# Causal attention and a ternary feed-forward layer on one core: the layout in which K and Q are kept in DRAM, and where some loads stand in the queue

## The chip, the core and the metric

The kernel runs on one core of one Trainium2 chip, as one program with one launch. The metric is the device time of that program in microseconds: the median of several executions. One further execution is recorded by the hardware profiler; its page and its trace are what the prediction is argued from.

## The reference

The input is one sequence of 4096 tokens with 256 features. There are 16 heads of 16 features each, causal. All is float32.

```python
xn  = layernorm(x) * gamma + beta
q, k, v = split(xn @ w_qkv.T)                 # each 4096 x 256, 16 heads of 16
sim = (q * 16**-0.5) @ k.T                    # per head, masked above the diagonal
x   = layernorm(x + softmax(sim) @ v)         # heads side by side again
h   = silu(x @ w1.T * s1) * (x @ w2.T * s2)   # 256 -> 1024
h   = gelu(h @ h1.T * sh1)                    # 1024 -> 1024
h   = gelu(h @ h2.T * sh2)                    # 1024 -> 1024
out = layernorm(x + h @ w3.T * s3)            # 1024 -> 256
```

The feed-forward weights are ternary (times a constant); the scales s1, s2, sh1, sh2 (1024 numbers each) and s3 (256) multiply each output feature.

## The kernel before

**Precision.** [...] A value that has to keep its precision is split into a high part (the rounded value) and a low part (what the rounding left out), and a product is the sum of high times high, low times high and high times low. For a head, K and Q have 16 rows (features) each, so one matmul does all three products at once when the rows are stacked: for Q the rows are high, low, high; for K they are high, high, low. That is 48 rows. Two more rows hold ones for K and, for Q, the negative row maximum as a high and a low row (called hl), so that the maximum is subtracted inside the scores' matmul. With them there are 50 rows (`KR`).

**Stages.** The tokens are cut into 8 blocks of 512. `projections` makes Q, K and V of a block and stores them in DRAM: `qaug[b]` (16 heads x 48 rows x 512 tokens), `kaug[b]` (16 x 50 x 512) and `vaug[b]`. The high part is stored twice, since it stands in the stack twice; line 269 issues these stores, three of 16 rows for each half of the heads. Line 274 stores K's two rows of ones. For block 0 the stores go around over three queues (ACT, SP, POOL), afterwards all are issued by POOL.

**Attention.** For each query block (in the order 0, 1, 2, 3, 4, 6, 7, 5) and each group of four heads (`qd`) there is a step. `row_max` goes over the key blocks once for the maxima: matmuls at line 442, and VectorE's reduction at line 453. Its last part, `rows`, turns the maxima and writes the hl rows into the Q tile with four small DMAs (line 469). `scores` goes over the key blocks a second time: matmuls at line 486, the exponential on ScalarE at line 490. `product` multiplies with V at line 504. The two passes run interleaved, the maxima some steps ahead.

Both passes read their K tiles from DRAM through `fetch`. A K tile has 128 partitions: two halves of 64, each with two heads side by side along its free dimension, and of each half the first 50 rows are filled, by one DMA from SP's queue (line 410). For the scores a V tile comes along (line 416). The tiles of the maxima are called mk, those of the scores sk, and there are two buffers of each, so that one tile is read while the next is loaded. The Q tile (qt, line 429) is loaded once for a step, 48 rows to each half.

**Feed-forward.** While attention goes on, the feed-forward layer of finished blocks is worked off in pieces between the attention matmuls: `feed`, with up to two blocks at work, started by `start(b)`. `start` loads the block's x (line 672, tile x1) and its attention output (line 681), and lets `total` add them some turns later. Weight tiles (wt, line 665) are loaded through POOL's queue. The last block goes through `closing` when attention is done.

**Order.** The order of the instructions on TensorE, VectorE, ScalarE and POOL is that of the program text, fixed by `in_order` with dependencies that carry no wait. DMA issues are left out of that order: the scheduler places them by itself, and one that waits for nothing can move ahead. A dependency added by `after` holds one instruction behind another in the same way, without a wait between them on the chip. The scales are loaded by `scales()`, called in the text just before attention starts; on the chip these loads stand among SP's first, at 1.83 us, and so do the x1 load of block 0 (10.16 us) and the eight stores of ones (from 11.39 us).

Of the kernel before, what the change touches and what calls it, by code (L numbers as in the profile page):

```python
# [7 lines left out]
F32 = mybir.dt.float32  # L8
FR = mybir.dt.float32r
AF = mybir.ActivationFunctionType  # L10
ALU = mybir.AluOpType
# [4 lines left out]
N, E, H, D = 4096, 256, 16, 16  # L16
# [4 lines left out]
B = 512  # L21
NB = N // B
NQ = H // 4
KR = 50
# [19 lines left out]
def tokens(ap):  # L44
    return ap.rearrange("(t p) e -> p t e", p=P)


class Layer:
    def __init__(self, tc, a):
        self.tc, self.nc, self.a = tc, tc.nc, a  # L50
        self.last = {}

    def pool(self, ctx, name, bufs=1, **kw):
        return ctx.enter_context(self.tc.tile_pool(name=name, bufs=bufs, reuse_waits="tile", **kw))
# [20 lines left out]
    def chain(self, key):  # L75
# [3 lines left out]
            self.after(inst, self.last[key])  # L79
        self.last[key] = inst.name  # L80

    def run(self):
        tc, nc, a = self.tc, self.nc, self.a
        with ExitStack() as ctx:
            dram = self.pool(ctx, "dram", space=DRAM)
            cst = self.pool(ctx, "cst")
            self.small = self.pool(ctx, "small", 4)
            self.qaug = [dram.tile([H, 48, B], F32, name=f"qaug{b}") for b in range(NB)]
            self.kaug = [dram.tile([H, KR, B], F32, name=f"kaug{b}") for b in range(NB)]
            self.vaug = [dram.tile([NQ, P, 4, 4, D + 1], F32, name=f"vaug{b}") for b in range(NB)]  # L90
            self.attn = [dram.tile([B, E], F32, name=f"attn{b}") for b in range(NB)]

            self.ident = cst.tile([P, P], F32, name="ident")
            make_identity(nc, self.ident)
            self.mhalf = cst.tile([P, 4], F32, name="mhalf")
            nc.gpsimd.memset(self.mhalf, -0.5)
            self.wbad = cst.tile([P, 22], F32, name="wbad")
            self.wseq = (
                [("glu", g, 0) for g in range(4)]
                + [(n, g, k) for n in ("h1T", "h2T") for g in range(4) for k in range(2)]  # L100
                + [("w3T", 0, k) for k in range(2)]
            )
            self.sc = {}
            for n in ("w1_s", "w2_s", "h1_s", "h2_s"):
                self.sc[n] = cst.tile([P, 8], F32, name=n)
            self.w1_half = cst.tile([P, 8], F32, name="w1_half")
            self.w12 = cst.tile([P, 8], F32, name="w12")
            self.s3 = cst.tile([P, E], F32, name="s3")

            own = mybir.EngineType  # L110
            with ExitStack() as fctx, self.in_order(own.PE, own.DVE, own.Activation, own.Pool):
                self.layer(fctx)
            bad = self.verdict(cst)
            with tc.If(bad > 0), ExitStack() as gctx:
                self.general(gctx)

    def scales(self):
        for n, t in self.sc.items():
            self.nc.sync.dma_start(t, self.a[n].rearrange("(c p) -> p c", p=P))
        self.nc.gpsimd.tensor_scalar(self.w1_half, self.sc["w1_s"], 0.5, None, ALU.mult)  # L120
        self.nc.gpsimd.tensor_tensor(self.w12, self.w1_half, self.sc["w2_s"], ALU.mult)
        s3 = self.a["w3_s"].rearrange("(o f) -> o f", o=1)
        self.nc.sync.dma_start(self.s3, s3.broadcast_to([P, E]))

    def norm_steps(self, dst, src):

# [73 lines left out]
    def projections(self, ctx):  # L200
# [5 lines left out]
        one = self.pool(ctx, "p1", side="right")  # L206
        wk = self.pool(ctx, "pw", 2, side="right")

        def fetch(b):
            xb = wk.tile([P, 4, E], F32, name="xb")  # L210
            nc.sync.dma_start(xb, tokens(a["x"][b * B : (b + 1) * B]))
            return xb

        def front(b, xb):
# [37 lines left out]
        for b in range(NB):  # L252
            xh, xl = parts.pop(b)
            prods = [(wh, xh, c) for c in range(2)] + [(wl, xh, c) for c in range(2)] + [(wh, xl, c) for c in range(2)]
            for off, dst, order in ((E, self.kaug, (0, 0, 1)), (0, self.qaug, (0, 1, 0))):
                kp = ps.tile([P, 2, B], F32, name="s", tag="s", bufs=3)
                for T in range(2):
                    for n, (wp, xp, c) in enumerate(prods):
                        nc.tensor.matmul(  # L259
                            kp[:, T], wp[:, c, off + T * P : off + (T + 1) * P], xp[:, c], start=n == 0, stop=n == 5  # L260
                        )
                kh = wk.tile([P, 2, B], FR, name="kh")
                nc.scalar.copy(kh, kp)
                kl = wk.tile([P, 2, B], FR, name="kl")
                nc.vector.tensor_tensor(kl, kp, kh.bitcast(F32), ALU.subtract)
                for n, (i, g) in enumerate(sorted((i, g) for g, i in enumerate(order))):
                    for T in range(2):
                        queues = (nc.scalar, nc.sync, nc.gpsimd) if b == 0 else (nc.gpsimd,)
                        queues[(2 * n + T) % len(queues)].dma_start(
                            dst[b][8 * T : 8 * T + 8, 16 * g : 16 * g + 16, :], (kh, kl)[i][:, T].bitcast(F32)  # L270
                        )
                yield 12 * MM, True
                if dst is self.kaug:
                    nc.sync.dma_start(self.kaug[b][:, 48:KR, :], ones)
                    if b + 1 < NB:
                        yield from front(b + 1, xb)
                        if b + 2 < NB:
                            xb = fetch(b + 2)
            if b + 2 < NB:
                self.layernorm(xb, xb)  # L280
            v = vst[b % 2]
            vps = ps.tile([P, 4, E], F32, name="s", tag="s", bufs=3)
            for t in range(4):
                for n, (wp, xp, c) in enumerate(prods):
                    nc.tensor.matmul(
                        vps[:, t], xp[:, c, t * P : (t + 1) * P], wp[:, c, 2 * E :], start=n == 0, stop=n == 5
                    )
            for t in range(4):
                nc.scalar.copy(v[:, :, t, :, 0:D], vps[:, t].rearrange("p (q h d) -> p q h d", q=NQ, d=D))
            nc.gpsimd.dma_start(  # L290
                self.vaug[b].rearrange("q p t h d -> p q (t h d)"), v.rearrange("p q t h d -> p q (t h d)")
            )
            self.projected = b
            yield 12 * MM, True

    def layer(self, ctx):
# [92 lines left out]
        nc.vector.tensor_copy(tri, tri_f)  # L389
        opsum = ps.tile([P, B], F32, name="opsum")  # L390
        nc.vector.memset(opsum, 0.0)
        self.scales()

        steps = [(qb, qd) for qb in ORDER for qd in range(NQ)]
        order = {
# [5 lines left out]
        def fetch(kind, key):  # L401

            seq = order[kind]
            j = seq.index(key)
            while loaded[kind] < min(j + 2, len(seq)) and seq[loaded[kind]][2] <= self.projected:
                qb, qd, kb = nxt = seq[loaded[kind]]
                kt = (mk if kind == "m" else sk).tile([P, 2, B], FR, name=kind + "k")
                for e in range(2):
                    hs = slice(4 * qd + e, 4 * qd + 4, 2)
                    nc.sync.dma_start(  # L410
                        kt[half * e : half * e + KR].bitcast(F32), self.kaug[kb][hs].rearrange("r p t -> p r t")
                    )
                vt = None
                if kind == "s":
                    vt = sk.tile([P, 4, 4, D + 1], F32, name="vk")
                    nc.sync.dma_start(
                        vt.rearrange("p t h d -> p (t h d)"), self.vaug[kb][qd].rearrange("p t h d -> p (t h d)")
                    )
                tiles[kind, nxt] = kt, vt
                loaded[kind] += 1  # L420
            return tiles[kind, key]
# [3 lines left out]
        def row_max(qb, qd):  # L425
            qt = qtile[qb, qd] = qp.tile([P, 2, B], FR, name="qt")
            for e in range(2):
                hs = slice(4 * qd + e, 4 * qd + 4, 2)
                nc.sync.dma_start(
                    qt[half * e : half * e + 48].bitcast(F32), self.qaug[qb][hs].rearrange("r p t -> p r t")  # L430
                )
            mp = small.tile([P, 2, 2, 4, NB], F32, name="mp")
            nc.gpsimd.memset(mp, NEG)
            for kb in range(qb + 1):
# [234 lines left out]
    def load(self, b):  # L669
        self.live += 1  # L670
        x1 = self.fk.tile([P, 4, E], F32, name="x1", bufs=3)
        self.nc.sync.dma_start(x1, tokens(self.a["x"][b * B : (b + 1) * B]))
        return x1

    def start(self, b):

        nc = self.nc
        self.busy.add("at")
        x1 = self.load(b)
        at = self.fk.tile([P, 4, E], F32, name="at")  # L680
        nc.sync.dma_start(at, tokens(self.attn[b]))

        def total():
            nc.gpsimd.tensor_tensor(x1, x1, at, ALU.add)
            self.free("at")

        self.defer("next", total, 7)
        for delay, step in self.norm_steps(x1, x1):
# [392 lines left out]
```

## Time and profile before

| | |
|---|---|
| median of 3 executions | 2467.73 us (2458.92 to 2470.17) |
| profiled execution | 2476.85 us, its span 2475.1 us |
| TensorE (PE) busy | 2259.4 us, 91% of the span |
| VectorE (DVE) busy | 1567.3 us, 63% |
| ScalarE (ACT) busy | 1394.0 us, 56% |
| POOL busy | 714.2 us, 29% |
| DMA | 310.02 MB, mean 125 GB/s |
| K loads (mk and sk, line 410) | 288 and 288, 200 KB each, from SP |
| Q loads (line 429) | 64, 192 KB each, from SP |
| hl rows (line 469) | 128, 4 KB each, from SP |
| granted TensorE clock | 0.933 of full speed |

The span is the time from the first instruction to the last. Busy is the time in which an engine had an instruction at work; for TensorE its end is modelled, so 91% does not say that the array is used to its peak. The waits tell for each instruction that came after idle time of its engine what it waited for; SPq is SP's queue of DMA issues, PEq TensorE's sequencer. In the table by stretches of time, DMA share is the mean busy share of the core's 16 DMA engines.

### The profile page before, as it was taken

To read this page: it belongs to the slowest core of one execution; us is meant where nothing else is said; L and a number is where in the kernel's file an instruction comes from. 1 tells how busy PE (TensorE), PEld (TensorE's weight loads), DVE (VectorE), ACT (ScalarE), POOL (GpSimd) and SP (SyncE) were. 2 spreads that over 40 slices of the span, in tenths; PEclk is the share of its full clock that TensorE was granted. 3 is DMA by queue.
4 is the path that set the end of the run, shared out by engine and by line. 5 is a ranking of instruction groups with operands and counts; after the bars stand their busy time and mean duration, and the time that the engine had idled before them with its cause. 6 is when DMAs were issued, how large, how long until landed. Compare 5 with 4: busy or idle time off the path is not lost.

```text
span 2475.1 us, 36371 instructions
## 1 busy us (share of the span) xinstructions
PE 2259.4 (91%) x13986; PEld 1216.6 (49%) x13986; DVE 1567.3 (63%) x1826; ACT 1394.0 (56%) x1698; POOL 714.2 (29%) x1021
## 2 busy tenths in 40 slices
PE   4677899999998999999899999999999999999888
PEld 3545444545455544545445544554445443454366
DVE  3445687566656667576766677666766467755553
ACT  2242556545655566556665666566666677656731
POOL 2342413143223143131423132131423131313421
PEclk8687889969999989989999989999899999999999
DMA  7776834434643634535354544545354533454933
GB/s 185 200 175 158 192 101 116 121 80 121 128 111 92 156 103 108 129 97 141 103 123 109 139 95 105 132 109 139 80 127 111 142 108 101 110 111 131 243 94 86
DMA packets 251811, 310.02 MB, mean 125 GB/s; under 512 B 41328, under 2 KB 179696, under 8 KB 251632
## 3 DMA queue, kind: packets, MB, share of 16 engines
q1 hardware_dynamic: 141920, 184.87, 26.9%
q0 software_dynamic: 108352, 120.91, 22.6%
q8 instruction: 113, 1.85, 0.3%
q10 hardware_dynamic: 1360, 1.84, 0.2%
q14 instruction: 66, 0.54, 0.1%
HBM read 268.45 MB, written 38.54 MB: 124 GB/s over the span
## 4 chain that ended last, share of the span: by engine, by line
PE 67%; DVE 16%; ACT 7%; DMA 5%; issue 3%; POOL 2%; SPq 0%; ACTq 0%; POOLq 0%; DVEq 0%
PE m L830 17%; PE opsum L504 15%; PE s L486 11%; DVE mp L453 11%; PE s L442 10%; PE m L802 4%; ACT p L490 4%; PE bank L931 2%; PE m L857 2%; PE s L259 2%; PE s L449 1%; DMA qt<-hl 1%; DVE th L806 1%; ACT th L805 1%; DMA mk<-h2T_in 1%
## 5 line engine op out<-in xcount | busy, mean ns | idle before, releaser
L453 DVE TENSOR_REDUCE mp<-s 128x2 f32<-128x1024 f32 (+3 forms) x1152 | 1265.4, 1132 | 560.6 <-PE s L442 404.6
L490 ACT ACTIVATE p<-s 128x1024 f32<-128x1024 f32 (+3 forms) x1152 | 1062.9, 954 | 677.1 <-PE s L486 665.6
L486 PE MATMUL s<-qt,sk 50*128 50x512 f32 (+3 forms) x2304 | 514.6, 452 | 86.2 <-DVE mp L453 46.4
L442 PE MATMUL s<-mk,qt 48*128 48x512 f32 (+3 forms) x2304 | 513.9, 448 | 57.1 <-DVE mp L453 18.4
L504 PE MATMUL opsum<-p,vk 128*17 128x512 f32 (+3 forms) x4608 | 557.0, 586 | 2.8 <-POOL p L493 2.6
L830 PE MATMUL m<-act,wt 128*128 128x512 f32 x1792 | 477.1, 408 | 0.7 <-DVE xl L785 0.7
L486 PEld LDWEIGHTS s<-qt,sk 50*128 50x128 f32 x2304 | 223.1, 193 | 400.5 <-DVE mp L453 141.5
L830 PEld LDWEIGHTS m<-act,wt 128*128 128x128 f32 x1792 | 321.8, 189 | 123.8 <-issue 53.1
L442 PEld LDWEIGHTS s<-mk,qt 48*128 48x128 f32 x2304 | 229.8, 197 | 307.0 <-ACT p L490 134.6
L504 PEld LDWEIGHTS opsum<-p,vk 128*17 128x17 f32 x4608 | 97.7, 98 | 234.1 <-issue 214.1
L493 POOL TENSOR_SCALAR_AFFINE_SELECT p<-p 128x256 f32<-128x256 f32 x256 | 105.1, 420 | 292.1 <-ACT p L490 290.9
L665 POOL DMA_DIRECT2D wt<-h1T_in x64 | 48.9, 764 | 378.9 <-PE m L830 231.0
L665 POOL DMA_DIRECT2D wt<-h2T_in x64 | 49.4, 772 | 366.0 <-PE m L830 310.9
L755 POOL TENSOR_TENSOR act<-raw,act 128x512 fp32r<-128x512 f32 x112 | 145.1, 1295 | 8.9
L838 ACT ACTIVATE raw<-m,h_s 128x512 f32<-128x512 f32 x112 | 77.1, 689 | 107.5 <-PE m L830 107.5
L802 PE MATMUL m<-xh,wt 128*128 128x512 f32 x224 | 105.9, 473 | 11.9 <-DVE th L806 9.1
L449 PEld LDWEIGHTS s<-tri,pick 64*128 64x128 f32 x1024 | 96.1, 205 | 7.2
L802 PE MATMUL m<-xl,wt 128*128 128x512 f32 x224 | 93.3, 416 | 0.0
L449 PE MATMUL s<-tri,pick 64*128 64x128 f32 (+1 forms) x1024 | 88.4, 252 | 0.0
L754 POOL CAST act<-raw 128x512 fp32r<-128x512 f32 x112 | 70.9, 633 | 41.9 <-ACT raw L759 41.9
L754 POOL CAST act<-th 128x512 fp32r<-128x512 f32 x56 | 34.4, 614 | 144.6 <-DVE th L808 144.3
L806 DVE SCALAR_TENSOR_TENSOR th<-th,m 128x512 f32<-128x512 f32 x56 | 38.4, 686 | 55.2 <-ACT th L805 55.1
(126 smaller groups left out, 1530.2 us busy)
## 6 DMA issues: line engine op xcount, KB each, us to landing
mk<-kaug SPq DMA_DIRECT2D x288, 200.0 KB
sk<-kaug SPq DMA_DIRECT2D x288, 200.0 KB
wt<-h1T_in POOLq DMA_DIRECT2D x64, 512.0 KB, 4.3
wt<-h2T_in POOLq DMA_DIRECT2D x64, 512.0 KB, 4.2
vk<-vaug SPq DMA_DIRECT2D x144, 136.0 KB
qt<-qaug SPq DMA_DIRECT2D x64, 192.0 KB
wt<-w1T_in POOLq DMA_DIRECT2D x34, 256.0 KB, 4.2
wt<-w2T_in POOLq DMA_DIRECT2D x34, 256.0 KB, 5.2
```

Of the source, the lines that this page charges most:

```text
L442: nc.tensor.matmul(m[:, e, :k1], qt[rows, r, t * P : (t + 1) * P], kt[rows, r, :k1], start=True, stop=kb != qb,)
L449: nc.tensor.matmul(m[:, e, k1 - P + half * i : k1], pick[rows, i], tri[rows, : P - half * i], start=False, stop=i == 1,)
L453: nc.vector.tensor_reduce(mp[:, r, :, t, kb], m[:, :, :k1], AX.X, ALU.max)
L486: nc.tensor.matmul(s[:, e, lo:], kt[rows, r, t * P : (t + 1) * P], qt[rows, r, lo:], start=True, stop=True)
L490: nc.scalar.activation(p[:, :, lo:], s[:, :, lo:], AF.Exp, scale=0.25)
L493: nc.gpsimd.affine_select(out=p[:, :, lo : lo + P], in_=p[:, :, lo : lo + P], compare_op=ALU.is_ge, fill=0.0, base=0, pattern=[[0, 2], [1, ...
L504: nc.tensor.matmul(opsum[32 * j : 32 * j + D + 1, lo:], vt[:, t, j], pt[j // 2][:, j % 2, lo:], start=first, stop=last,)
L665: self.nc.gpsimd.dma_start(dst, src)
L754: nc.gpsimd.tensor_copy(hi, src)
L755: nc.gpsimd.tensor_tensor(lo, src, hi.bitcast(F32), ALU.subtract)
L802: nc.tensor.matmul(s, wt[:, 2 * i + k, cols], x[:, k], start=k == n == 0, stop=k == n == 1)
L830: nc.tensor.matmul(s, wts[k // 4][:, k % 4, cols], x[:, k % 4], start=k == n == 0, stop=k == 7 and n == 1)
```

## The change

Three things change.

The stacks in DRAM hold the high parts a single time. `qaug[b]` has 32 rows for a head (high, low) in place of 48; `kaug[b]` has 34 (high, low, ones) in place of 50. The stack in the tile stays the same and is put together by the loads, each half by two DMAs through the new helper `rows`. For K these are 16 rows (high) and then all 34 (high, low, ones) behind them. For Q they are all 32 (high, low) and then 16 (high). So there are four loads for a K tile and for a Q tile where there were two. The stores of a block are 8 in place of 12. For block 0 the three queues now take them by the number `2 * i + T`: the high parts go to ACT and SP, the low parts to POOL and ACT.

The scales are loaded when the first feed-forward block starts, and the two small POOL operations on them stand in its `total`.

Some loads get places in SP's queue: the scales and the x1 loads are held behind the newest K or V load of attention issued in the text (`mark`, `held`), and the store of ones of a block behind the load of that block's x (`loads`).

```diff
@@ class Layer
+        self.mark = None
+    def held(self):
+        if self.mark:
+            self.after(self.nc.cur_bb.bb.instructions[-1], self.mark)
@@ run
-            self.qaug = [dram.tile([H, 48, B], F32, name=f"qaug{b}") for b in range(NB)]
-            self.kaug = [dram.tile([H, KR, B], F32, name=f"kaug{b}") for b in range(NB)]
+            self.qaug = [dram.tile([H, 32, B], F32, name=f"qaug{b}") for b in range(NB)]
+            self.kaug = [dram.tile([H, 34, B], F32, name=f"kaug{b}") for b in range(NB)]
+    def rows(self, dst, first, src):
+        n = src.shape[1]
+        self.nc.sync.dma_start(dst[first : first + n].bitcast(F32), src.rearrange("r p t -> p r t"))
     def scales(self):
         for n, t in self.sc.items():
             self.nc.sync.dma_start(t, self.a[n].rearrange("(c p) -> p c", p=P))
-        self.nc.gpsimd.tensor_scalar(self.w1_half, self.sc["w1_s"], 0.5, None, ALU.mult)
-        self.nc.gpsimd.tensor_tensor(self.w12, self.w1_half, self.sc["w2_s"], ALU.mult)
+            self.held()
         s3 = self.a["w3_s"].rearrange("(o f) -> o f", o=1)
         self.nc.sync.dma_start(self.s3, s3.broadcast_to([P, E]))
+        self.held()
@@ projections
+        loads = {}
         def fetch(b):
             xb = wk.tile([P, 4, E], F32, name="xb")
             nc.sync.dma_start(xb, tokens(a["x"][b * B : (b + 1) * B]))
+            loads[b] = nc.cur_bb.bb.instructions[-1].name
             return xb
...
-            for off, dst, order in ((E, self.kaug, (0, 0, 1)), (0, self.qaug, (0, 1, 0))):
+            for off, dst in ((E, self.kaug), (0, self.qaug)):
...
-                for n, (i, g) in enumerate(sorted((i, g) for g, i in enumerate(order))):
+                for i, part in enumerate((kh, kl)):
                     for T in range(2):
                         queues = (nc.scalar, nc.sync, nc.gpsimd) if b == 0 else (nc.gpsimd,)
-                        queues[(2 * n + T) % len(queues)].dma_start(
-                            dst[b][8 * T : 8 * T + 8, 16 * g : 16 * g + 16, :], (kh, kl)[i][:, T].bitcast(F32)
+                        queues[(2 * i + T) % len(queues)].dma_start(
+                            dst[b][8 * T : 8 * T + 8, 16 * i : 16 * i + 16, :], part[:, T].bitcast(F32)
                         )
                 if dst is self.kaug:
-                    nc.sync.dma_start(self.kaug[b][:, 48:KR, :], ones)
+                    nc.sync.dma_start(self.kaug[b][:, 32:34, :], ones)
+                    self.after(nc.cur_bb.bb.instructions[-1], loads[b])
@@ layer
-        self.scales()
@@ layer, fetch
                 for e in range(2):
                     hs = slice(4 * qd + e, 4 * qd + 4, 2)
-                    nc.sync.dma_start(
-                        kt[half * e : half * e + KR].bitcast(F32), self.kaug[kb][hs].rearrange("r p t -> p r t")
-                    )
+                    self.rows(kt, half * e, self.kaug[kb][hs, 0:16])
+                    self.rows(kt, half * e + 16, self.kaug[kb][hs])
...
+                self.mark = nc.cur_bb.bb.instructions[-1].name
@@ layer, row_max
-                nc.sync.dma_start(
-                    qt[half * e : half * e + 48].bitcast(F32), self.qaug[qb][hs].rearrange("r p t -> p r t")
-                )
+                self.rows(qt, half * e, self.qaug[qb][hs])
+                self.rows(qt, half * e + 32, self.qaug[qb][hs, 0:16])
@@ load
         self.nc.sync.dma_start(x1, tokens(self.a["x"][b * B : (b + 1) * B]))
+        self.held()
@@ start
+        if b == ORDER[0]:
+            self.scales()
         x1 = self.load(b)
...
         def total():
             nc.gpsimd.tensor_tensor(x1, x1, at, ALU.add)
             self.free("at")
+            if b == ORDER[0]:
+                nc.gpsimd.tensor_scalar(self.w1_half, self.sc["w1_s"], 0.5, None, ALU.mult)
+                nc.gpsimd.tensor_tensor(self.w12, self.w1_half, self.sc["w2_s"], ALU.mult)
```

## The prediction

> **What bounds the kernel now.** I read the page first, for the engines' shares and the slices of the span.
>
> ```profile
> PE 2259.4 (91%) x13986; PEld 1216.6 (49%) x13986; DVE 1567.3 (63%) x1826; ACT 1394.0 (56%) x1698; POOL 714.2 (29%) x1021
> ...
> PE   4677899999998999999899999999999999999888
> ```
>
> From the fifth slice on TensorE is nearly always busy; only the first 250 us have holes. The waits say what the holes are. TensorE waits for a K load for almost nothing, and for a Q load or a row maximum (hl) in few places; the long waits are other engines waiting for TensorE.
>
> ```profile
> ACT p L490 <- PE s L486: 665.6, 550, 9.2
> DVE mp L453 <- PE s L442: 404.6, 351, 9.9
> ...
> PE s L486 <- DMA qt<-hl: 16.5, 5, 4.3
> PE s L442 <- DMA qt<-qaug: 15.8, 2, 15.2
> PE s L486 <- DMA sk<-kaug: 1.5, 2, 0.8
> ```
>
> So K loads are hidden, and the question is by how much. SP's own waits and its timeline answer: SP sits until a K buffer is read out, issues at once, and the tile has the life of its neighbour (12 to 16 us between loads of one kind) to land.
>
> ```profile
> SPq L410 <- PE s L486: 544.9, 126, 18.4
> SPq L410 <- PE s L442: 406.2, 92, 13.3
> ```
> ```profile
> 1307.41 0.67 SPq L410 DMA_DIRECT2D sk<-kaug  x2
> 1310.34 0.67 SPq L410 DMA_DIRECT2D mk<-kaug  x2
> ...
> 1322.76 0.67 SPq L410 DMA_DIRECT2D mk<-kaug  x2
> 1325.92 0.67 SPq L410 DMA_DIRECT2D sk<-kaug  x2
> ```
>
> Last, stretches of 0.2 us around one pair of K loads that ran alone (issued at 540.61 and 540.94), then around one V load (128 rows), then the steady stage. The last two columns are the mean busy share of 16 DMA engines and GB/s.
>
> ```profile
> 542.40:542.60 0.20, 0.20 (x2) 0.18 (x1) 0.20 (x1) 0.00 (x0) 0.00 (x0) 0.50 0.66 256
> 543.00:543.20 0.20, 0.20 (x2) 0.17 (x1) 0.20 (x1) 0.00 (x0) 0.00 (x0) 0.50 0.64 195
> 543.20:543.40 0.20, 0.20 (x2) 0.13 (x1) 0.10 (x1) 0.00 (x0) 0.00 (x0) 0.50 0.68 215
> ```
> ```profile
> 2087.60:2087.80 0.20, 0.20 (x8) 0.20 (x6) 0.00 (x0) 0.00 (x0) 0.00 (x0) 1.00 0.90 218
> ```
> ```profile
> 270.00:2275.00 2005.00, 1902.15 (x12005) 974.97 (x12004) 1345.15 (x1450) 1215.08 (x1431) 562.98 (x778) 0.95 0.47 115
> ```
>
> The V load keeps nearly all engines busy (0.90). The 50-row K loads stop at 0.64 to 0.68, which is ten of sixteen (0.63) and a little: five rows on each of ten engines. Both loads of the pair do, and the second follows the first on no more engines, so both sit on the same ten. One engine then moves 25.6 GB/s at best and 19.5 to 21.5 in the second load.
>
> **The K read, 50 rows in two pieces of 16 and 34.** Per tile and half there were 50 rows x 2 heads x 2 KB on ten engines, 10 packets each. 16 rows split evenly over 16 engines: 2 packets each. 34 rows split evenly over two engines and no larger number up to sixteen. If they are split as 50 rows were, two engines carry 17 rows x 2 heads = 34 packets each. Nothing in this trace moves 34 rows, so the ends are 2 engines (even split) and 12 (three rows each, uneven). I take 2, since the 50-row load, which could have had four rows on each of 13 engines, took ten.
>
> [...]
>
> Now the two engines' work in the steady stage, 270 to 2275 us (2005 us). The line's own query counts 530 K loads there (268 for the maxima, 262 for the scores). Each now brings such an engine 36 packets of 2 KB, 73.7 KB; 39.1 MB in all. At 25.6 GB/s that is 1526 us, at the 20.5 of the second load 1906; halfway, 23 GB/s, 1700. The rest: 115 GB/s x 2005 us = 231 MB, less 530 x 204.8 KB = 109 MB, leaves 122 MB, 7.6 MB an engine. At 25.6 GB/s that is 298 us, the low end. By busy share it is more: 0.47 x 2005 = 942 us, less 265 pairs x 1.29 us (the shares of that pair added up over its stretches) = 342, leaves 600. Halfway, 449.
>
> So these two engines have 1824, 2149 or 2506 us of work in 2005 us. Loads of both kinds, V, Q, hl and weights all need them, and at most one tile of each kind is ahead. In the middle case TensorE waits until the stage is as long as the two engines' work: **+145 us** (ends 0 and +501). The low end leaves them 91% full, with stalls that the spacing of 12 to 16 us may hide.
>
> **Issue and waits of the pieces.** 576 more K issues and 64 more for Q (both Q pieces, 32 and 16 rows, split evenly over 16) at 0.34 us: 218 us of SP, which waits over 950 us for K buffers; a tile is issued 0.7 us later. TensorE's sequencer gets up to 640 more waits; those at these lines take 51 ns, so 0 to 33 us, and as they run ahead of the array I take +2. Without the cover of one tile ahead all of this would lie on the path.
>
> **The hl rows.** Four small DMAs a step queue on SP behind K pieces on the two engines: up to two loads, 2 x 3.2 us. In the first 260 us, where hl makes 10.4% of the chain (27 us, four waits of 6 to 9 us or so), each may pay it. 0 to +26; I take +10. Later the scores start well behind the maxima, and waits were 16.5 us in all.
>
> **The start.** Now the last Q low part is queued on SP behind a K load that waits for its source:
>
> ```profile
> 46.34 0.33 SPq L410 DMA_DIRECT2D mk<-kaug  x1
> 46.72 3.11 SPq L269 DMA_DIRECT2D qaug<-kl  x1
> ```
>
> Its data was ready at 35.8; TensorE pays with its 15.2 us wait for the first Q tile. In the new order K's and Q's low parts of block 0 leave from POOL and ACT, so that block is gone. The gain lies between 0 and 15; the first K tile itself lands some 5 us later on two engines, so I take -11. Storing the high parts once removes 32 stores of 256 KB; 30 of them were on POOL at 0.60 us, 18 us beside a POOL that is 40% busy there (59 of 145 us). A few stand in the chain (1.1 to 1.8 us a group): 0 to -18, I take -4.
>
> **Held places.** The scales' five DMAs occupy SP from 1.83 to 10.1 us, where nothing needs it. At the first feed-forward block (about 244 us) behind them stand the attention load, K loads and hl: 0 to +8, I take +3. The x loads cost 0.4 us each and are wanted seven turns later; the two POOL operations move with the scales; the stores of ones (0.6 us each) now come one a block: zero, covered by those turns, and under 1 us each if late.
>
> **Sum.** Span 2475.1 + 145 + 2 + 10 - 11 - 4 + 3 = 2620; the execution was 1.75 us longer than its span, 2622. The profiled execution (2476.85) is 0.37% above the median of 2467.73, so by the median **2612**. Its own range: without the +145 it meets the first rival; all dear ends together (501, 33, 26, 8, no gains) give 3043, by the median 3032, of which I take the lower three quarters, up to 2890.
>
> **Rivals.** First, two engines, but hidden: the two halves of a tile take 2 x 36 packets, 5.8 to 7.2 us, in 12 to 16 us of spacing, and waiting TensorE is made up by VectorE and ScalarE that caught up. For it: today TensorE waits 1.5 us for K. Against: maxima and scores share the engines, 12 to 14 us in that spacing, before the rest's 15 to 30%. Sum without the 145: 2475, by the median 2468; with a few stalls up to 2500.
>
> Second, faster: 34 rows spread over 12 engines, or each load over two other engines. Then no engine fills up, the pieces cost only issues, and the start decides: no hl cost either, 2475.1 - 11 - 4 + 3 + 2 = 2465, by the median 2457; with the whole 15 and 18 us, 2439. It decides if three-row shares exist or the pair rotates; the ten-engine rows, both loads on the same ten, speak against both.
>
> **How the numbers follow.** Forecast 0.70, hidden 0.17, spread 0.13. About 0.5% (12 us) is what a measurement can tell from no change. Faster by more: 0.08 of the spread case and 0.01 of the hidden one, 0.09. Within: 0.05 and 0.09, 0.14. Slower: 0.70 and 0.07, 0.77. The range 2450 to 2890 leaves out some 0.06 below and 0.12 above; the forecast's own is 2490 to 2890.
>
> **What would show it.** In stretches around a lone K load: a busy share near 0.13 and 40 to 51 GB/s for 2.7 to 3.4 us. Among TensorE's waits: K tiles with over 100 us in total where there were 1.5. SP's waits for K buffers shorter. The first maxima before 60 us instead of 67.8. It is wrong if the share stays above 0.6, or if K waits stay under 20 us.

## The result and the profile after

The changed kernel takes 2779.45 us (median of 4; 2767.55 to 2790.06), the kernel before 2466.76 us on the same chip: a ratio of 1.127 (1.122 to 1.133), 313 us slower. The direction and the range held; the size is over twice the forecast 144 us. The profiled execution took 2767.55 us with a span of 2765.8.

The page after, its first part. TensorE has the same instructions, is busy 105 us longer (2364.3 for 2259.4) and idle 186 us longer.

```profile
PE 2364.3 (85%) x13986; PEld 1268.8 (46%) x13986; DVE 1572.7 (57%) x1826; ACT 1396.0 (50%) x1698; POOL 696.2 (25%) x991
```

Its waits (in all, times, longest): where TensorE waited 1.5 us for a scores' K tile, and 15.8 us for a Q tile, it now waits for both kinds of K tile and for Q, 219 us together. The hl rows are not what is late.

```profile
PE s L499 <- DMA sk<-kaug: 83.8, 31, 8.1
PE s L455 <- DMA mk<-kaug: 69.3, 33, 6.3
PE s L455 <- DMA qt<-qaug: 65.8, 10, 10.7
...
PE s L499 <- DMA qt<-hl: 5.7, 3, 4.0
```

SP's own waits have a kind that before did not have to any extent: SP waits for K loads to land (the trace tells a landing by the last update of the load's semaphore) before it issues the next DMA (line 126 is the helper `rows`), 213 us.

```profile
SPq L126 <- DMA sk<-kaug: 127.9, 77, 4.0
...
SPq L126 <- DMA mk<-kaug: 85.6, 42, 3.8
```

Stretches of 0.4 us around 1801 to 1805 us, while TensorE waits for a tile of the maxima. The last three columns are granted clock, busy share of the 16 DMA engines, GB/s. Where 50-row loads alone had 0.64 to 0.68, there is 0.14, two engines and a little; and 51 GB/s, 25.6 for each.

```profile
1801.20:1801.60 0.40, 0.39 (x1) 0.00 (x0) 0.36 (x1) 0.40 (x1) 0.40 (x1) 0.50 0.14 51
1802.80:1803.20 0.40, 0.00 (x0) 0.00 (x0) 0.00 (x0) 0.38 (x2) 0.40 (x1) 0.50 0.14 51
1804.40:1804.80 0.40, 0.40 (x3) 0.10 (x1) 0.00 (x0) 0.00 (x0) 0.32 (x2) 0.50 0.14 51
```

TensorE's timeline there: it waits for the two halves of one tile in turn. In square brackets stands the idle time before, and what ended it.

```profile
1800.83 0.76 PE L455 MATMUL s<-mk,qt 48*128 48x512 f32 x1 [2.11 <-DMA mk<-kaug]
1804.03 1.19 PE L455 MATMUL s<-mk,qt 48*128 48x512 f32 x3 [2.44 <-DMA mk<-kaug]
```

By the semaphores in the trace, the two 34-row loads that ended these waits were issued at 1788.29 and 1789.54 us and landed at 1800.69 and 1803.89, 12 and 14 us later. Other loads moved in between: a V load issued at 1787.44 landed at 1796.49, a weight load issued at 1790.61 at 1799.57. A few microseconds earlier 2 KB packets (a packet is here one row of one head) of K took turns with 1 KB packets of a weight load, and the two engines moved 46 GB/s in all, 23 each:

```profile
1796.80:1797.20 0.40, 0.40 (x4) 0.00 (x0) 0.40 (x2) 0.40 (x2) 0.08 (x1) 1.00 0.15 46
```

Over the whole run a 34-row load lands 9.4 us (maxima) and 9.7 us (scores) after its issue in the median, 13 to 14 us in one of ten. A 50-row load before took 3.8 us, and 6 in one of ten.

### The profile page after: what moved, and what is told of

It is laid out like the page before. It is cut to its first block, busy times and chain, and to the rows that moved or that the text cites. A ratio compares the mean times of both kernels' runs of the same rounds, so it can differ in the third digit from the quotient of the medians.

```text
span 2765.8 us, 37208 instructions
## 1 busy us (share of the span) xinstructions
PE 2364.3 (85%) x13986; PEld 1268.8 (46%) x13986; DVE 1572.7 (57%) x1826; ACT 1396.0 (50%) x1698; POOL 696.2 (25%) x991
## 4 chain that ended last, share of the span: by engine, by line
PE 48%; DMA 31%; DVE 10%; ACT 4%; SPq 3%; issue 2%; POOL 1%; ACTq 0%; POOLq 0%; DVEq 0%
DMA sk<-kaug 12%; PE m L849 11%; DMA mk<-kaug 11%; PE opsum L517 11%; PE s L455 8%; PE s L499 8%; DVE mp L466 6%; DMA qt<-qaug 3%; PE m L821 3%; SPq L126 2%; PE bank L950 2%; ACT p L503 2%; PE m L876 1%; PE s L273 1%; DMA vk<-vaug 1%
## 5 line engine op out<-in xcount | busy, mean ns | idle before, releaser
L455 PE MATMUL s<-mk,qt 48*128 48x512 f32 (+3 forms) x2304 | 551.2, 458 | 171.2 <-DMA mk<-kaug 69.3
L499 PE MATMUL s<-qt,sk 50*128 50x512 f32 (+3 forms) x2304 | 553.6, 464 | 159.7 <-DMA sk<-kaug 83.8
L517 PE MATMUL opsum<-p,vk 128*17 128x512 f32 (+3 forms) x4608 | 578.5, 606 | 1.3 <-POOL p L506 1.1
L849 PE MATMUL m<-act,wt 128*128 128x512 f32 x1792 | 503.6, 426 | 0.7 <-DVE xl L804 0.7
L499 PEld LDWEIGHTS s<-qt,sk 50*128 50x128 f32 x2304 | 243.3, 200 | 486.6 <-issue 203.9
L455 PEld LDWEIGHTS s<-mk,qt 48*128 48x128 f32 x2304 | 249.9, 203 | 438.3 <-issue 192.6
L849 PEld LDWEIGHTS m<-act,wt 128*128 128x128 f32 x1792 | 339.3, 200 | 134.7 <-issue 59.7
L462 PEld LDWEIGHTS s<-tri,pick 64*128 64x128 f32 x1024 | 102.0, 212 | 6.8
L462 PE MATMUL s<-tri,pick 64*128 64x64 f32 (+1 forms) x1024 | 94.2, 258 | 0.0
L774 POOL TENSOR_TENSOR act<-th,act 128x512 fp32r<-128x512 f32 x56 | 71.6, 1278 | 4.7
```

Of the source, the lines that this page charges most:

```text
L455: nc.tensor.matmul(m[:, e, :k1], qt[rows, r, t * P : (t + 1) * P], kt[rows, r, :k1], start=True, stop=kb != qb,)
L462: nc.tensor.matmul(m[:, e, k1 - P + half * i : k1], pick[rows, i], tri[rows, : P - half * i], start=False, stop=i == 1,)
L499: nc.tensor.matmul(s[:, e, lo:], kt[rows, r, t * P : (t + 1) * P], qt[rows, r, lo:], start=True, stop=True)
L517: nc.tensor.matmul(opsum[32 * j : 32 * j + D + 1, lo:], vt[:, t, j], pt[j // 2][:, j % 2, lo:], start=first, stop=last,)
L774: nc.gpsimd.tensor_tensor(lo, src, hi.bitcast(F32), ALU.subtract)
L849: nc.tensor.matmul(s, wts[k // 4][:, k % 4, cols], x[:, k % 4], start=k == n == 0, stop=k == 7 and n == 1)
```

## The experiments

Times are medians, each compared with runs of the kernel before on the same chip (2466 to 2473 us).

**36 rows in K's store: 12 engines.**

```diff
-            self.kaug = [dram.tile([H, 34, B], F32, name=f"kaug{b}") for b in range(NB)]
+            self.kaug = [dram.tile([H, 36, B], F32, name=f"kaug{b}") for b in range(NB)]
...
-        ones = one.tile([32, B], F32, name="ones")
+        ones = one.tile([64, B], F32, name="ones")
...
-                    nc.sync.dma_start(self.kaug[b][:, 32:34, :], ones)
+                    nc.sync.dma_start(self.kaug[b][:, 32:36, :], ones)
```

> The changed kernel with 36 rows of a head in K's store (four rows of ones in place of two; the two more are loaded and never read), so the second piece of a K load has 36 rows. Same number of DMAs as the change, a few more bytes. Theory (two engines carry the 34-row pieces): 36 rows split evenly over 12 engines, the most loaded engine gets 6 + 2 packets a load in place of 34 + 2, and the loss goes: 2440 to 2470 us, waits of TensorE for K under 20 us, a busy share near 0.75 around a lone K load. Rival (twice as many DMAs on the eight semaphores that SP's DMAs take in turn, so that SP waits for landings): the count is the same, so 2700 us or more.

2470.63 us, ratio 1.0009 (0.9984 to 1.0033). Two rows more in the store, and the whole loss is gone. TensorE's waits for K tiles are a few us again, and so are SP's waits for landings:

```profile
PE s L499 <- DMA sk<-kaug: 5.3, 2, 4.0
...
PE s L455 <- DMA mk<-kaug: 3.0, 2, 2.3
```
```profile
SPq L126 <- DMA sk<-kaug: 2.9, 6, 1.0
```

So everything else in the change together is worth nothing that this can measure.

**35 rows: 7 engines.** The same edit with 35 and 48.

> The changed kernel with 35 rows of a head in K's store (three rows of ones), so the second piece has 35 rows: one row more than the change. Theory (even split): 35 splits over 7 engines, 10 + 2 packets a load on each, about as much as before (10): 2440 to 2480 us. Rival (rows are shared out three to an engine, or the number of rows does not matter): 34 and 35 rows would be alike, 2770 us.

2472.45 us, ratio 0.999 (0.9965 to 1.0015). 34 rows and 35 rows differ by 307 us. The number of such packets on SP's queue at one time, counted from the trace's packet records, is most often 2 with 34 rows (1453 us), 7 with 35 (303 us), 12 with 36 (113 us) and 10 before (263 us). Each of these numbers divides its rows evenly, and from 34 rows to 35 or 36, with nothing else changed, the loss goes.

**Only the read cut in two.**

```diff
-                    nc.sync.dma_start(
-                        kt[half * e : half * e + KR].bitcast(F32), self.kaug[kb][hs].rearrange("r p t -> p r t")
-                    )
+                    for a, z in ((0, 16), (16, KR)):
+                        nc.sync.dma_start(
+                            kt[half * e + a : half * e + z].bitcast(F32),
+                            self.kaug[kb][hs, a:z].rearrange("r p t -> p r t"),
+                        )
```

> The kernel before, with K's store of 50 rows, and only line 410 cut in two: rows 0 to 15 and rows 16 to 49. Stores, scales, Q loads and places are those of before. Theory (the read in 16 and 34 rows is the whole loss): 2750 to 2820 us, a little above the change, because the start is not shortened. Rival (the loss is in the moved loads, the scales or Q's two pieces): 2460 to 2500 us.

2773.92 us, ratio 1.121 (1.113 to 1.128). The loss without any other part of the change.

**Twice the DMAs on ten engines.**

```diff
-                    nc.sync.dma_start(
-                        kt[half * e : half * e + KR].bitcast(F32), self.kaug[kb][hs].rearrange("r p t -> p r t")
-                    )
+                    for r in range(2):
+                        nc.sync.dma_start(
+                            kt[half * e : half * e + KR, r].bitcast(F32), self.kaug[kb][4 * qd + e + 2 * r]
+                        )
```

> The kernel before with each 50-row K load cut by head: two DMAs of 50 rows x 2 KB, both still on ten engines. Twice as many K issues as before, the same bytes on the same engines. Theory (two engines): 2460 to 2485 us, at most 0.7% lost to issues. Rival (number of DMAs and the eight semaphores): 2650 us or more.

2467.85 us, ratio 0.9991 (0.9969 to 1.0013). Four DMAs a tile cost nothing here, where they land 3.2 us after their issue in the median.

These four show the cause, the 34-row piece on two engines, and leave the size. The next ones ask for it.

**Half the load on the two engines.**

```diff
-                    self.rows(kt, half * e + 16, self.kaug[kb][hs])
+                    self.rows(kt, half * e + 16, self.kaug[kb][hs, 0:32] if kind == "m" else self.kaug[kb][hs])
```

> The changed kernel, with the second piece of the maxima's tiles cut to 32 rows (they never use the rows of ones): 16 engines. The scores' tiles keep 34 rows on two engines. Theory (the two engines' load decides): their K work falls to little over half, some 55% of the time with all the rest, so TensorE hardly waits: 2480 to 2540 us, not half of the loss. If the loss were simply proportional to the number of 34-row loads: 2625 us. Granted clock back above 0.92.

2534.77 us, ratio 1.027 (1.021 to 1.034). A fifth of the loss for half the load, so not proportional; but 62 us is also not the nothing that "the engines are not full" would make it. It keeps four DMAs a tile, so the 62 us are not those of the two engines' load alone.

**32 rows and 2 rows.** The same with `hs, 0:32` for both kinds, and for the scores a third piece, `self.rows(kt, half * e + 48, self.kaug[kb][hs, 32:34])`.

> The changed kernel, with the 34 rows of a scores' tile cut into 32 (16 engines) and 2 (two engines, two packets each), and 32 for the maxima: ten DMAs for a pair of tiles in place of eight, none long. Theory: 2460 to 2485 us, SP's waits for landings near zero although there are more DMAs than semaphores. Rival (number of DMAs): over 2500 us.

2502.43 us, ratio 1.013 (1.007 to 1.019). A miss on the theory's side: no load is long, TensorE's direct waits for K are under 7 us and SP's waits for K to land 11 us, but ten DMAs a pair of tiles still cost about 30 us. TensorE's waits for the Q tile are 32.7 us, where the kernel with 36 rows has 16.4; where the rest goes was not found.

**One piece, shorter matmuls.** K's store read by `self.rows(kt, half * e, self.kaug[kb][hs])` alone, the matmuls over 32 and 34 rows.

> The changed kernel with K's 34 rows as the only piece of a K tile and Q's 32 rows as the only piece of a Q tile, products over 32 and 34 rows: two DMAs a tile as before the change, each on two engines with 34 packets (36 with the change). Leaves out the cross products of high and low parts. It asks why the loss was 291 us of span where 145 stood in the sum. Theory A (SP, held until the eighth DMA before has landed, issues late, so the two engines run dry): with half the DMAs the hold goes, 2560 to 2650 us, SP's waits for landings under 40 us. Theory B (the packets on the two engines alone, slower than assumed): 2720 to 2750 us.

> The same with 38 rows in K's store (six of ones): one piece of 38 rows, two engines, 38 packets each, so that this and the 34-row one stand on both sides of the change's 36. Same parts of the product left out. Theory A: 2640 to 2740 us. Theory B: 2810 to 2840 us. If 38 rows used more engines, 2480 us.

2844.61 and 2907.95 us (the second from 2875.53 to 2940.18). Both theories missed. TensorE waits 25 us for the scores' K tiles, and yet it is busy 2665 us at a clock of 0.867:

```profile
PE 2665.2 (94%) x13986; PEld 1326.8 (47%) x13986; DVE 1586.6 (56%) x1826; ACT 1401.1 (49%) x1698; POOL 693.8 (24%) x991
```

The maxima's matmuls take 521 ns on average in place of 448 before. Busy time times clock is 2311 us, where it is 2111 with the change, so the clock is not all of it. With the fewer rows in the matmul TensorE's own time was another, so these two runs say nothing about DMAs. The next ones keep 48 and 50 rows.

**One piece, matmuls as before.** In the two kernels with one piece, persistent K tiles, zeroed once, so that the 16 rows that are not loaded can be read; the weights' check left out in all three.

```diff
-                kt = (mk if kind == "m" else sk).tile([P, 2, B], FR, name=kind + "k")
+                kt = keep[kind][loaded[kind] % 2]
...
-                    self.rows(kt, half * e, self.kaug[kb][hs, 0:16])
...
-                self.inspect(mk)
+                nc.vector.memset(self.wbad, 0.0)
```

> Control for the next two: the changed kernel without the weights' check at the end (the 22 loads and comparisons of inspect, left out with their result). 2690 to 2770 us.

> As the control, with the 16-row piece of K not loaded (those rows stay zero; the product of the high parts is left out) and all matmuls over 48 and 50 rows as in the change, which the earlier one-piece run did not keep. Two K DMAs a tile, 34 packets on each of the two engines in place of 36. It asks what the number of DMAs adds on the two engines. Theory A (SP waits for the landing of the eighth DMA before, so loads are issued late): 100 us or more below the control, SP's waits for landings under 40 us. Theory B (packets alone): 40 to 60 us below.

> The same with 38 rows in K's store, one piece of 38 rows, 38 packets on each of the two engines. Theory A: still below the control by 40 us or more. Theory B: 40 to 60 us above it.

Control 2757.63 us; 34 packets 2572.75 us; 38 packets 2700.77 us. The control has 36 packets on each of the two engines; halfway between the other two is 2637, so **two DMAs a tile in place of four are worth 121 us at the same load** of the two engines, and a packet more or less is worth 32 us. Theory A in size and sign. SP's waits for K to land fall as well, from 205 us in the control to 50, though not under the 40 that were expected:

```profile
SPq L126 <- DMA sk<-kaug: 123.4, 65, 4.9
...
SPq L126 <- DMA mk<-kaug: 81.9, 45, 4.1
```
```profile
SPq L126 <- DMA sk<-kaug: 36.9, 23, 2.6
...
SPq L126 <- DMA mk<-kaug: 13.3, 10, 2.8
```

The one-piece kernels also begin their maxima later, at 66.3 and 69.3 us where the control does at 52.6, so 121 us may be some 15 us too little. From the trace: between the release of a maxima's buffer and the last of its K issues pass 3.1 us in the median and 9.7 us in one of ten in the control, 0.4 and 2.7 us with one piece of 34 rows (0.4 and 1.7 before the change). A late issue is not a loss by itself: the kernel with 36 rows has 2.7 and 7.1 us and loses nothing. There a 36-row piece lands 3.3 us after its issue in the median, in the control a 34-row piece some 9 us.

**Tiny DMAs in place of the second piece.**

```diff
+                    nc.sync.dma_start(
+                        kt[half * e + 56 : half * e + 57, 0, 0:16].bitcast(F32), self.kaug[kb][4 * qd + e, 0:1, 0:16]
+                    )
                     self.rows(kt, half * e + 16, self.kaug[kb][hs])
```

> The one-piece kernel with 34 rows (2573 us, product of the high parts and weights' check left out) with one more DMA of 64 bytes ahead of each K piece, into a row that no matmul reads: four K DMAs a tile again as in the change, with the long ones and their packets unchanged. It asks whether the 120 us between one and two pieces come from the number of DMAs (eight semaphores in turn on SP's queue, each reused only when its last DMA has landed) or from the 16-row piece's own packets. Number: 2660 to 2760 us, SP's waits for landings over 120 us again. Packets: 2565 to 2590 us.

2681.29 us, 109 us above the same kernel without them. 64 bytes beside the 136 KB of a piece are next to no load, so here it is the number of DMAs that costs. SP's waits for landings are back, 319 us, now mostly ahead of the tiny DMA (line 429), against the 50 us in the kernel without:

```profile
SPq L429 <- DMA mk<-kaug: 127.7, 51, 5.4
SPq L429 <- DMA sk<-kaug: 122.9, 51, 8.1
...
SPq L126 <- DMA mk<-kaug: 36.7, 21, 3.2
```

The trace points at the reason. SP's 1016 DMAs before and 1654 after use eight semaphores in turn, each some 127 and 207 times, and ahead of 938 and 1617 of them SP waits for the very semaphore that the DMA will use; none was issued before the DMA that had its semaphore last had landed. Eight DMAs are four tiles' loads at two a tile, and two tiles' at four. No run changes the number of semaphores, so that the hold is the whole of the 109 us is read from SP's waits and not shown.

**TensorE made to wait without any DMA.**

```diff
-                        nc.vector.tensor_reduce(mp[:, r, :, t, kb], m[:, :, :k1], AX.X, ALU.max)
+                        for _ in range(2 if t % 2 == 0 else 1):
+                            nc.vector.tensor_reduce(mp[:, r, :, t, kb], m[:, :, :k1], AX.X, ALU.max)
```

> The kernel before, with the reduction of the maxima done twice in every second tile of queries (same result, some 650 us more of VectorE; no DMA is changed). TensorE then waits for VectorE. It asks whether TensorE's lower clock in the changed kernel (0.893 for 0.933, 105 us more busy time for the same matmuls) comes from its waiting as such. If so: 2560 to 2750 us, granted clock under 0.915 and TensorE's busy time over 2300 us. If the clock has another cause: 0.93 and 2260 us.

2876.68 us, slower than expected, and the clock 0.887:

```profile
PE 2441.5 (85%) x13986; PEld 1271.2 (44%) x13986; DVE 2186.7 (76%) x2402; ACT 1412.2 (49%) x1698; POOL 710.3 (25%) x1021
```

The DMAs are those of before, TensorE's matmuls too, and it is busy 182 us longer; half clock on its busy time, 542 us where it was 281, makes 130 of them. Idle 219 us longer than before, TensorE ran slower between its waits (granted clock 0.887 for 0.933). This run alone does not part the waiting from the added work of VectorE, but in the changed kernel the clock falls with VectorE's work as before (1572.7 us for 1567.3). Nor does every wait cost this: the kernel with half the load is idle 46 us longer than the one before, at the same granted clock (0.933).

**The start alone.** Kernel before, `queues[(2 * n + T + n // 2) % len(queues)]` for block 0's stores.

> The kernel before, with block 0's low parts stored from POOL and ACT in place of SP and POOL; nothing else. It takes the start's gain alone, the block of the last Q low part behind a waiting K load. By the sum 11 us less: 2457 us; the first maxima 10 to 15 us earlier. If the gain is given back later, as the kernels with 35 and 36 rows say: 2465 to 2475 us.

2465.32 us, ratio 0.998 (0.9962 to 0.9997) in five rounds: about 5 us, the second expectation at its low end, the only version that is faster than both kernels, at the edge of what can be told. The first maxima come 8.5 us earlier.

## Why the prediction was right in direction and short in size

**The two engines: right.** The 34-row loads ran on two engines: the share where only such loads run is 0.14 (0.13 forecast), TensorE's waits for K passed 100 us (153), SP's waits for K buffers became shorter (642 us for 951 at the two lines of matmuls), and the first maxima start at 52.7 us (before 60 forecast). By the packets in flight the runs showed 2, 7, 10 and 12 engines for 34, 35, 50 and 36 rows.

**Their price: near in size, in part by luck.** The sum took 23 GB/s an engine, halfway between two readings; they do 25.6 where K loads alone run, the sum's cheap end, at which its term is near zero, and 23 beside a weight load. The one-piece runs put the term at +168 us (2637 against 2468). They leave out the weights' check, which the kernel before has and which is worth about 22 us in the changed kernel, so it may be that much more. The sum's assumption was that TensorE waits only once the engines' work is longer than the stage. In the sum's middle case it gives 49, 145 and 237 us for 34, 36 and 38 packets a load (an estimate with the sum's own numbers); the runs with one piece, against the kernel before, give 104, 168 (halfway) and 232. So the loss grows by 32 us a packet and not 47, and begins earlier. How full the two engines were is not told, since the packet records do not name the engine. From the load of the eleventh scores' tile to the last, exactly two packets were in flight for 1037 of 2288 us (39 of 2028 before), and fewer than two for 106 (841 before), so both were at work for at most 95% of it.

**Issue and waits of the pieces: the step that failed.** The sum had +2 us, for an issue 0.7 us later and some waits of the sequencer. It measured +121 us by the one-piece runs and +109 by the tiny DMAs. SP's queue was looked at for its time, not for how many DMAs it has in flight; by the trace's semaphores and SP's waits, what held it was the landing of the eighth DMA before (1634 of the 1654 came eight places behind the last one on their semaphore). On ten engines that hold did not bite (four DMAs a tile, landing 3.2 us after their issue in the median, 7 us of SP's waits for K at the line of the loads, no loss); with the 34-row loads, which landed after 9.4 and 9.7 us in the median, SP waited 213 us for landings. The 168, the 121 and the 22 us of the check add up to the distance of 311 us by construction, each being the difference of two neighbouring kernels; what the check is worth in the kernel before no run shows.

**What a wait costs: not in the sum.** It counted waits as idle time alone. Of the 291 us of span only 186 are idle time; 105 are the same matmuls taking longer. These 105 are no further term beside the 168 and 121; they are part of them, seen another way. Busy time times granted clock is 2108 us before (2259.4 x 0.933) and 2111 after (2364.3 x 0.893): the work is nearly unchanged. By the trace's clock records the clock is granted in full or by half; half for 333 us in 41 stretches before and for 596 us in 78 after, in multiples of 3.41 us. On busy time of TensorE fall 281 and 467 us of it, which makes 93 of the 105. The falls came with short idle stretches of TensorE: the clock fell at 1800 us, in the wait of 2.1 us above and after one of 1.0 us, and of the 78 falls after the change 73 had no idle stretch of over 3.4 us in the 3.41 us ahead of them, nor had any of the 41 before. What makes the clock fall no run shows.

**The hl rows: wrong place.** +10 us was taken; the waits for hl fell from 16.5 us at line 486 to 5.7, although the hl rows landed later, 4.2 us after their issue in the median for 2.2 before. It is the Q tile's loads that came late, 65.8 us for 15.8.

**Start and held places.** The first maxima came 15.2 us earlier (11 taken), and in the kernels with 35 and 36 rows 13 to 15 us earlier. Their medians show none of it at the end, while the start's edit alone keeps some 5 us. Where the rest is given back was not found: run-to-run differences are of that size. The scales, the x loads and the ones cost nothing that shows beside the start's gain in the kernel with 36 rows.

## What to carry to other kernels

When a DMA is cut or its row count changed, look at how the count divides: here 34 rows ran on two engines and cost 307 us more than 35, which ran on seven, and padding with rows that nobody reads was free in comparison. Count DMAs in flight as well as their issue time: with the eight semaphores in turn that SP's queue had here, twice the DMAs was half the look-ahead in tiles. Twice the DMAs cost 109 to 121 us where landings took 9 us and nothing where they took 3, though ten DMAs for a pair of tiles cost some 30 us even without a long load. And TensorE's waits cost more here than their length: beside 186 us more of idle time the same matmuls took 105 us longer, at a granted clock of 0.893 for 0.933.

## What the runs showed of the hardware that was not expected

- One engine moved 25.6 GB/s in 2 KB packets whether two ran (51 GB/s) or ten (256 GB/s in the first load of a pair); the slower second load of a pair, 195 to 215 GB/s, was not a limit of the single engine. With 1 KB packets of a weight load in between it moved 23.
- Matmuls over 32 and 34 rows in place of 48 and 50 went with a granted clock of 0.867 (756 us at half clock by the clock records) although TensorE was busy 94% of the span. The half clock makes 216 of the 406 us that it was busy longer than in the kernel before; why it fell, and what the rest is, was not tried further.
- Twice the reduction in every second tile made 619 us more work for VectorE (2186.7 against 1567.3), which was busy 63% of the span before; it cost 401 us of span (2475.1 to 2876.1), 182 of it in longer busy time of TensorE, of which the lower clock makes some 130.
